# When the attention accumulator takes its PSUM slot, and in which order the second query half visits its key tiles

## The chip, the cores and the metric

The kernel runs on one core of a Trainium2 chip. Five engines work from queues of their own, each in the order in which its instructions were written into the program: TensorE (PE, matrix products and transposes; PEld is its loading of the stationary operand), VectorE (DVE), ScalarE (ACT), GpSimd (POOL) and SyncE (SP, which here only starts DMA transfers). They wait for each other through semaphores. The metric is the time of one execution on the device in microseconds; lower is better.

## The reference

A transformer block in float32 over x of shape (8, 1024, 512): eight batch elements of 1024 tokens. It has two residual branches, each with a layer norm before and after:

```python
x = x + layernorm(attention(layernorm(x)))
x = x + layernorm(feed_forward(layernorm(x)))
```

Attention has 16 heads of 32 columns and a causal mask: q, v, k come from one projection, the weights are softmax((q k^T masked) / sqrt(512)), and the weighted values go through an output projection. The feed-forward part expands 512 to 2048 columns, applies `relu(h + c * w * sin(theta + 0.1 h))` with per-column parameters, and goes back to 512.

## The kernel before

All batch elements are worked one after the other. In each, the 16 heads are taken in four groups of four (`NG`, `HPG`), since four heads of 32 columns fill the 128 rows of TensorE. The tokens are cut into eight tiles of 128 and into two query halves of 512, called `c` in the code.

One head group has two stages. `find_maxima` (line 354) computes scores in nine units, from which DVE takes the row maxima under the causal mask (lines 395 and 400); between its units it lets TensorE advance the projections of the next group (`work`, made by `project_qkv`, tiles `pq` and `pv`). Then `attention` (line 534) walks the ten units of `KEY_UNITS` (line 349): three for the first query half, seven for the second. A unit is one key tile, or two that together fit in 512 columns. For each unit `weigh` (line 430) does this:

- TensorE writes minus the maximum and then the product of keys and queries into two `st` tiles (two heads each).
- ACT takes the exponential into two `w` tiles (line 466) and with that frees the `st` tiles.
- For a key tile on the diagonal, POOL puts zeros where the mask is, one instruction for each `w` tile and each such key tile (line 470). In the first half all units have such tiles: 0, 1 and 3, 2. In the second half these are 4, 5 and 7, 6; key tiles 0 to 3 lie wholly in the past and have none.

The products of a unit with the values (`weighted_values`, line 483) are held back in `late` and issued by `flush`, after the scores of the next unit. They are summed up in a PSUM tile `acc`, plane 0. Plane 1 takes the sums of the weights. In the first half TensorE makes these with a matrix of ones, unit by unit (`weight_sums`, line 496). In the second half DVE adds the weights of all later units onto those of the first one (`add_weights`, line 509; the pair is called `total`), and one sum matmul over this total follows after the scores of the next group's first unit (`sums`). `normalise` (line 516) then divides: DVE transposes the sums, ACT copies the values out and frees `acc`, DVE inverts and multiplies.

PSUM is handled by hand (line 75): four slots of two banks each in a list. A tile takes the slot at the head of the list (`psum`), and puts it at the end when its last reader has been issued (`drained`). So the list fixes, at the time the program is written, which earlier tile's reader a new tile must wait for. Besides `st` and `acc`, the tiles `sc` (scores for the maxima), `pq`, `pv`, `parts_t`, `y`, `xn_t`, `ph` and `ys` all go through this list.

TensorE's queue keeps the order of the source (`keep_in_program_order`), and so do POOL's masks and variance roots (lines 210 and 211). DVE's and ACT's instructions are placed into their queues by the framework's planner when the program is built.

`attention` also runs other work between its units (`more`, from `after` on line 753): in group 0 the rest of the previous element's second residual; in group 2 the first layer norm of the next element (`norm1`: loads into `xin`, statistics, scale, transposes `xn_t`, copies to `xnT`); in group 3, from the second half's second unit on, the first half's `finish_block` (output projection `y`, residual, layer norm, transposes, copies to `x2T`). The feed-forward part follows; its first `ph` matmul reads `x2T`.

The twenty `w` tiles of a group share seven buffers (`pp`), which the feed-forward part uses too.

Of the kernel before, what the change touches and what calls it, by code (L numbers as in the profile page):

```python
# [16 lines left out]
P = 128  # L17
# [14 lines left out]
def kernel(  # L32
# [21 lines left out]
    HALF = 512  # L54
# [23 lines left out]
    def psum(shape, name, dtype=F32):  # L78
        slot = free_slots.pop(0)
        t = ps.tile(shape, dtype, tag=f"s{slot}", name=name)  # L80
        slot_of[id(t)] = slot, t
        return t

    def drained(t):

        free_slots.append(slot_of.pop(id(t))[0])

    def matmul(*args, **kwargs):
        tc.keep_in_program_order(nc.tensor.matmul(*args, **kwargs))  # L89
# [177 lines left out]
    def advance(work, steps=1):  # L267
        for _ in range(steps):
            if next(work, None) is None:
                return  # L270

    def finish(work):
        for _ in work:
            pass
# [26 lines left out]
    def project_qkv(b, g):  # L301


        qk[b, g] = qkp.tile([P, 2, S], F32, tag="qk", name=f"qk_{b}_{g}")
        v[b, g] = vp.tile([P, NT, P], F32, tag="v", name=f"v_{b}_{g}")
        for half in range(2):
            pq = psum([P, 2, HALF], "pq")
            for n, part in enumerate((0, 2)):
                c0 = part * D + g * P
                for kc in range(KC):  # L310
                    matmul(
                        pq[:, n, :],
                        wqvk_sb[:, kc, c0 : c0 + P],
                        xnT[b, half][:, kc, :],
                        start=(kc == 0),
                        stop=(kc == KC - 1),
                    )
                    if kc % 2 and (n, kc) != (1, KC - 1):
                        yield True
            tok = slice(half * HALF, (half + 1) * HALF)  # L320
            nc.scalar.activation(qk[b, g][:, 0, tok], pq[:, 0, :], AF.Copy, scale=QSCALE)
            nc.scalar.copy(qk[b, g][:, 1, tok], pq[:, 1, :])
            drained(pq)
            yield True
        pv = psum([P, NT, P], "pv")
        c0 = D + g * P
        for t in range(NT):
            for kc in range(KC):
                matmul(
                    pv[:, t, :],  # L330
                    xnT[b, t // TPB][:, kc, (t % TPB) * P : (t % TPB + 1) * P],
                    wqvk_sb[:, kc, c0 : c0 + P],
                    start=(kc == 0),
                    stop=(kc == KC - 1),
                )
            if t % 2 and t < NT - 1:
                yield True
        nc.scalar.copy(v[b, g], pv)
        drained(pv)
        yield True  # L340
# [7 lines left out]

    KEY_UNITS = (
        ((0,), (1, 3), (2,)),  # L350
        ((0,), (1,), (2,), (3,), (4,), (5, 7), (6,)),
    )

    def find_maxima(b, g, work, sums):
# [128 lines left out]
    def weighted_values(acc, b, g, first, last, weights, placed):  # L483

        for k, (kb, cols, n) in enumerate(placed):
            for j in range(HPG):
                r = slice(j * HD, (j + 1) * HD)
                matmul(
                    acc[r, 0, HALF - n :],
                    v[b, g][:, kb, r],  # L490
                    weights[j // 2][:, j % 2, cols],
                    start=first and k == 0,
                    stop=last and k == len(placed) - 1,
                )

    def weight_sums(acc, first, last, weights, placed):

        for k, (_, cols, n) in enumerate(placed):
            for j in range(HPG):
                r = slice(j * HD, (j + 1) * HD)  # L500
                matmul(
                    acc[r, 1, HALF - n :],
                    ones,
                    weights[j // 2][:, j % 2, cols],
                    start=first and k == 0,
                    stop=last and k == len(placed) - 1,
                )
# [8 lines left out]
    def normalise(acc, dst):  # L516

        sums = tmp.tile([P, HALF], F32, tag="tmp", name="sums")  # L520
        nc.vector.transpose(sums, acc[:, 1, :])
        nc.scalar.copy(dst, acc[:, 0, :])
        drained(acc)
        yield True
        rinv = small.tile([P, HALF // HD], F32, tag="rinv", name="rinv", bufs=2)
        nc.vector.reciprocal(rinv, sums.rearrange("p (n r) -> p n r", r=HD)[:, :, 0])
        nc.vector.transpose(
            sums.rearrange("p (n r) -> p n r", r=HD),
            rinv.unsqueeze(2).to_broadcast([P, HALF // HD, HD]),
        )  # L530
        nc.vector.tensor_tensor(dst, dst, sums, ALU.mult)
        yield True

    def attention(b, wvT, after):


        late = [None]
        summing = [None]

        def flush():  # L540
            if late[0] is not None:
                late[0]()
                late[0] = None

        def sums():
            if summing[0] is not None:
                summing[0]()
                summing[0] = None

        def projections(g):  # L550
            if g + 1 < NG:
                return project_qkv(b, g + 1)
            if g + 1 == NG and b + 1 < B:
                return project_qkv(b + 1, 0)
            return iter(())

        rests = []

        def settle():
            while rests:  # L560
                finish(rests.pop(0))

        work = projections(0)
        for g in range(NG):
            mTs = [find_maxima(b, g, work, sums)]
            more, first = after(g)
            at = 0
            for c in range(2):
                acc = total = None
                units = KEY_UNITS[c]  # L570
                for u, keys in enumerate(units):
                    weights, placed = weigh(b, g, c, keys, mTs[c])
                    if at == 0:
                        advance(work)
                    if at == 2:
                        mTs.append(transpose_maxima(parts_q[1], nc.vector.tensor_copy))
                    flush()
                    if at:
                        settle()
                    if acc is None:  # L580
                        acc = psum([P, 2, HALF], "acc")

                    if c and u == 0:
                        total = weights, placed
                    elif c:
                        add_weights(total[0], weights, placed)

                    def divide(acc=acc, dst=wvT[c][:, g, :]):  # L590
                        rests.append(normalise(acc, dst))
                        advance(rests[-1])

                    def step(acc=acc, u=u, last=u == len(units) - 1, weights=weights,
                             placed=placed, c=c, g=g, total=total, divide=divide):
                        weighted_values(acc, b, g, u == 0, last, weights, placed)
                        if c == 0:
                            weight_sums(acc, u == 0, last, weights, placed)
                            if last:
                                divide()  # L600
                        elif last:

                            def whole():
                                weight_sums(acc, True, True, *total)
                                divide()

                            summing[0] = whole

                    late[0] = step
                    if at >= first:  # L610
                        advance(more)
                    at += 1
            finish(work)
            work = projections(g + 1)
            advance(work)
            flush()
            if g == NG - 1:
                advance(more)
                sums()
                settle()  # L620
            finish(more)
# [127 lines left out]
    for b in range(B):  # L749
        wvT = [tp.tile([P, KC, HALF], F32, tag="t", name=f"wvT_{b}_{n}") for n in range(2)]  # L750
        x2T = {}

        def after(g, b=b, wvT=wvT, x2T=x2T, rest=rest):

            if g == 0:
                return rest, 1
            if g == NG - 2 and b + 1 < B:
                return norm1(b + 1, True), 0
            if g == NG - 1:
                return finish_block(b, 0, wvT[0], x2T), len(KEY_UNITS[0]) + 1  # L760
            return iter(()), 0
# [47 lines left out]
```

## Time and profile before

| what | value |
|---|---|
| median of three runs | 4212.27 us (4211.95 to 4212.37) |
| the profiled execution's own time | 4213.73 us |
| its span | 4212.0 us |
| busy: PE, DVE, ACT, POOL | 4041.7, 3025.1, 1151.1, 533.1 us |
| mean granted TensorE clock | 0.991 |

The profile is of one execution. A line of its list of groups names the source line and engine, the operation, what it writes and reads, the shapes and the count; then busy time and the mean duration in ns; then the idle time of the engine just before, and what ended it. A line of a timeline gives start and length in us from the span's start, then the engine, line and operation; what stands in brackets at its end is the idle time before it and the instruction that ended it. Matmuls are recorded by one helper (line 89; transposes line 92), so they are told apart by their tiles: `st`, `acc<-w,v`, `acc<-w,ones`, `sc`, `pq`. A table of stretches gives, for each, its length, the busy time of PE, PEld, DVE, ACT and POOL with instruction counts, the granted TensorE clock, the share of DMA and its GB/s.

### The profile page before, as it was taken

How to read it: one execution, taken by the hardware profiler on the slowest of the kernel's cores; microseconds unless marked ns; L12 is line 12 of the kernel's file. 1: busy time of each engine (PE TensorE's matmuls, PEld its weight loads, DVE VectorE, ACT ScalarE, POOL GpSimd, SP SyncE). 2: the span in 40 equal slices, each digit the busy share in tenths (PEclk: the TensorE clock that was granted, in tenths of full speed). 3: DMA queues.
4: the chain of work that ended last, by engine and by line, in shares of the span. 5: the costliest groups of instructions: out<-in, count | busy, mean ns of one | idle time of the engine just before them, and what ended most of it. 6: DMA issues, size and time to landing. Idle time of an engine off the chain costs nothing.

```text
span 4212.0 us, 51995 instructions
## 1 busy us (share of the span) xinstructions
PE 4041.7 (96%) x20481; PEld 1802.6 (43%) x20481; DVE 3025.1 (72%) x6473; ACT 1151.1 (27%) x1564; POOL 533.1 (13%) x1037
## 2 busy tenths in 40 slices
PE   8999999999999999999999999999999999999998
PEld 4434444344443444444444444444444444443343
DVE  5776777766777677776677766777677776777666
ACT  3332123321233212332123321233212432123311
POOL 1121011200112001120011200112001210011100
PEclk9999999999999999999999999999999999999899
DMA  3000000000000000000000000000000000000000
GB/s 138 6 11 10 20 26 7 20 1 20 28 11 13 1 20 28 11 14 1 20 28 14 11 0 20 28 14 11 0 20 28 14 11 0 20 21 11 1 3 18
DMA packets 35430, 71.79 MB, mean 17 GB/s; under 512 B 3248, under 2 KB 3312, under 8 KB 34672
## 3 DMA queue, kind: packets, MB, share of 16 engines
q1 hardware_dynamic: 30992, 56.93, 4.1%
q10 hardware_dynamic: 4192, 11.53, 0.7%
q8 instruction: 160, 2.62, 0.3%
q14 instruction: 86, 0.70, 0.1%
HBM read 51.68 MB, written 16.78 MB: 16 GB/s over the span
## 4 chain that ended last, share of the span: by engine, by line
PE 82%; DVE 9%; POOL 4%; ACT 3%; issue 2%; DMA 0%; ACTq 0%; POOLq 0%; DVEq 0%; SPq 0%
PE ph L89 21%; PE ys L89 21%; PE pq L89 10%; PE sc L89 8%; PE st L89 7%; PE acc L89 6%; PE pv L89 5%; PE y L89 4%; ACT w L466 2%; POOL w L470 2%; DVE w L514 2%; DVE sc L400 1%; DVE st L204 1%; POOL rs L211 1%; PE xn_t L92 1%
## 5 line engine op out<-in xcount | busy, mean ns | idle before, releaser
L89 PE MATMUL ph<-x2T,w_sb 128*128 128x512 f32 x2048 | 921.1, 593 | 12.1 <-ACT hid L682 6.7
L89 PE MATMUL ys<-w_sb,hid 128*128 128x512 f32 x1536 | 691.1, 592 | 0.0
L466 ACT ACTIVATE w<-st 128x1024 f32<-128x1024 f32 (+1 forms) x640 | 565.8, 936 | 313.1 <-PE st L89 299.9
L89 PEld LDWEIGHTS ph<-x2T,w_sb 128*128 128x128 f32 x2048 | 385.3, 190 | 487.5 <-issue 466.8
L470 POOL TENSOR_SCALAR_AFFINE_SELECT w<-w 128x256 f32<-128x256 f32 x512 | 272.4, 553 | 2184.1 <-ACT w L466 2177.9
L400 DVE CUSTOM_DVE_ANT_0 sc<-sc,mask 128x512 f32<-128x512 f32 (+3 forms) x1024 | 487.5, 512 | 53.4 <-PE sc L89 38.9
L89 PE MATMUL pq<-xnT,wqvk_sb 128*128 128x512 f32 x1024 | 497.0, 614 | 1.3
L514 DVE TENSOR_TENSOR w<-w 128x1024 f32<-128x1024 f32 (+3 forms) x448 | 441.4, 1031 | 43.3 <-POOL w L470 29.6
L89 PEld LDWEIGHTS ys<-w_sb,hid 128*128 128x128 f32 x1536 | 291.2, 190 | 368.7 <-issue 341.9
L690 ACT ACTIVATE u<-u 128x512 f32<-128x512 f32 x256 | 161.1, 629 | 883.5 <-DVE u L175 883.4
L89 PE MATMUL sc<-qk 32*128 32x512 f32 (+3 forms) x3072 | 391.2, 529 | 10.3 <-DVE mx L400 6.1
L89 PE MATMUL acc<-w,v 128*32 128x512 f32 (+3 forms) x3072 | 363.8, 503 | 24.6 <-POOL w L470 24.6
L395 DVE TENSOR_REDUCE mx<-sc 128x2 f32<-128x1024 f32 x256 | 301.6, 1217 | 85.0 <-PE sc L89 85.0
L89 PE MATMUL st<-qk 32*128 32x512 f32 (+3 forms) x3072 | 348.8, 507 | 0.0
L685 DVE TENSOR_SCALAR u<-hid,prm 128x512 f32<-128x512 f32 x256 | 123.8, 484 | 292.5 <-ACT hid L682 292.5
L691 DVE SCALAR_TENSOR_TENSOR hid<-u,coef,hid 128x512 f32<-128x512 f32 x256 | 192.0, 750 | 174.0 <-ACT u L690 174.0
L682 ACT ACTIVATE hid<-ph,prm 128x512 f32<-128x512 f32 x256 | 175.4, 685 | 475.7 <-PE ph L89 475.7
L89 PEld LDWEIGHTS pq<-xnT,wqvk_sb 128*128 128x128 f32 x1024 | 176.6, 189 | 275.5 <-issue 247.0
L210 POOL TENSOR_SCALAR rs<-mv 128x1 f32<-128x1 f32 x256 | 78.2, 305 | 1468.3 <-DVE mv L205 1463.3
L89 PEld LDWEIGHTS pv<-wqvk_sb,xnT 128*128 128x128 f32 x2048 | 238.3, 192 | 47.8 <-issue 44.3
L89 PE MATMUL pv<-wqvk_sb,xnT 128*128 128x128 f32 x2048 | 254.4, 279 | 0.0
L89 PE MATMUL st<-mT,minus 32*128 32x512 bf16 (+3 forms) x1536 | 184.8, 333 | 56.4 <-ACT w L466 45.3
(90 smaller groups left out, 3592.9 us busy)
## 6 DMA issues: line engine op xcount, KB each, us to landing
x<-in_L_attn_h_dram SPq DMA_DIRECT2D x64, 256.0 KB, 2.7
out_dram<-x SPq DMA_DIRECT2D x64, 256.0 KB, 2.2
xin<-in_L_attn_h_dram SPq DMA_DIRECT2D x56, 256.0 KB, 2.7
w_tail<-in_L_ffn_W_dram SPq DMA_DIRECT2D x8, 1024.0 KB, 5.0
w_sb<-in_L_ffn_W_dram ACTq DMA_DIRECT2D x1, 4096.0 KB, 14.9
wqvk_sb<-in_L_attn_Wqvk_dram ACTq DMA_DIRECT2D x3, 1024.0 KB, 9.4
w_sb<-in_L_ffn_W_dram ACTq DMA_DIRECT2D x1, 3072.0 KB, 22.1
wo_sb<-in_L_attn_Wo_dram ACTq DMA_DIRECT2D x1, 1024.0 KB, 5.6
```

Source lines behind the costliest of these rows:

```text
L89: tc.keep_in_program_order(nc.tensor.matmul(*args, **kwargs))
L92: tc.keep_in_program_order(nc.tensor.transpose(*args))
L210: tc.keep_in_program_order(nc.gpsimd.tensor_scalar(rs, mv[:, :, 1], EPS, None, ALU.add))
L395: nc.vector.tensor_reduce(out=mx, in_=sc[:, :, cols], op=ALU.max, axis=mybir.AxisListType.X)
L400: nc.vector.tensor_tensor_reduce(out=sc[:, m, cols], in0=sc[:, m, cols], in1=mask[:, HALF - n :], scale=1.0, scalar=-FMAX, op0=ALU.add, op ...
L466: nc.scalar.activation(w[:, :, :width], st[:, :, :width], AF.Exp)
L470: select = nc.gpsimd.affine_select(out=square, in_=square, compare_op=ALU.is_ge, fill=0.0, base=0, pattern=[[0, 2], [1, P]], channel_multi ...
L514: nc.vector.tensor_add(t[:, :, q], t[:, :, q], w[:, :, cols])
L682: nc.scalar.activation(hid, ph, AF.Identity, bias=prm[:, fc : fc + 1])
L685: nc.vector.tensor_scalar(u, hid, 0.1, prm[:, NFC + fc : NFC + fc + 1], ALU.mult, ALU.add)
L690: nc.scalar.activation(u, u, AF.Sin)
L691: nc.vector.scalar_tensor_tensor(hid, u, coef[:, fc : fc + 1], hid, ALU.mult, ALU.add)
```

## The change

Two edits in the attention stage. The tuple of units for the second query half is reordered: the units with diagonal key tiles come first, the four full ones last. And `acc` is no longer taken from the slot list in the loop over units, before its first product is held back, but inside the held-back `step`, when the first unit's products are issued. That is one unit later: the scores of the second unit have taken their slots by then.

```diff
     KEY_UNITS = (
         ((0,), (1, 3), (2,)),
-        ((0,), (1,), (2,), (3,), (4,), (5, 7), (6,)),
+        ((4,), (5, 7), (6,), (0,), (1,), (2,), (3,)),
     )
...
             for c in range(2):
-                acc = total = None
+                accs = []
+                total = None
...
-                    if acc is None:
-                        acc = psum([P, 2, HALF], "acc")
...
-                    def divide(acc=acc, dst=wvT[c][:, g, :]):
-                        rests.append(normalise(acc, dst))
+                    def divide(accs=accs, dst=wvT[c][:, g, :]):
+                        rests.append(normalise(accs[0], dst))
                         advance(rests[-1])
 
-                    def step(acc=acc, u=u, last=u == len(units) - 1, weights=weights,
+                    def step(accs=accs, u=u, last=u == len(units) - 1, weights=weights,
                              placed=placed, c=c, g=g, total=total, divide=divide):
-                        weighted_values(acc, b, g, u == 0, last, weights, placed)
+                        if u == 0:
+                            accs.append(psum([P, 2, HALF], "acc"))
+                        weighted_values(accs[0], b, g, u == 0, last, weights, placed)
                         if c == 0:
-                            weight_sums(acc, u == 0, last, weights, placed)
+                            weight_sums(accs[0], u == 0, last, weights, placed)
                             if last:
                                 divide()
                         elif last:
 
                             def whole():
-                                weight_sums(acc, True, True, *total)
+                                weight_sums(accs[0], True, True, *total)
                                 divide()
 
                             summing[0] = whole
```

The first unit of the second half, whose weights become the total, is now key tile 4 instead of key tile 0. Both span all 512 columns of the half. Sizes and counts of all instructions are the same.

## The prediction

> **What bounds the kernel now.** I read the page first, then TensorE's timeline through one batch element, then the timelines of VectorE (DVE), GpSimd (POOL) and ScalarE (ACT) over the same stretches. TensorE's share on the page is so high that only its own gaps can be won:
>
> ```profile
> PE 4041.7 (96%) x20481; PEld 1802.6 (43%) x20481; DVE 3025.1 (72%) x6473; ACT 1151.1 (27%) x1564; POOL 533.1 (13%) x1037
> L89 PE MATMUL acc<-w,v 128*32 128x512 f32 (+3 forms) x3072 | 363.8, 503 | 24.6 <-POOL w L470 24.6
> L89 PE MATMUL st<-mT,minus 32*128 32x512 bf16 (+3 forms) x1536 | 184.8, 333 | 56.4 <-ACT w L466 45.3
> ```
>
> Batch elements repeat every 521.9 us, so one is enough. TensorE in head group 1 of the second one (weights stage from 660.09, next group's first score at 689.84), start and length in us:
>
> ```profile
> 662.74 0.34 PE L89 MATMUL st<-mT,minus 32*128 32x384 bf16 x2 [1.02 <-ACT w L466]
> ...
> 671.20 0.39 PE L89 MATMUL st<-mT,minus 32*128 32x512 bf16 x2
> 672.12 0.39 PE L89 MATMUL st<-mT,minus 32*128 32x512 bf16 x2 [0.52 <-ACT w L466]
> ...
> 682.59 1.87 PE L89 MATMUL acc<-w,v 128*32 128x512 f32 x8
> ...
> 686.37 1.06 PE L89 MATMUL acc<-w,v 128*32 128x384 f32 x12 [0.48 <-POOL w L470]
> ```
>
> The first two waits are for an exponential to free a score slot: four slots, one held by an accumulator that has no product yet. The 1.87 (undisturbed: 1.07) and the 0.48 are products of units (4) and (5, 7) waiting for POOL's masks. POOL and DVE there:
>
> ```profile
> 665.22 1.68 POOL L470 TENSOR_SCALAR_AFFINE_SELECT w<-w 128x256 f32<-128x256 f32 x4 [1.13 <-ACT w L466]
> ...
> 683.80 4.50 POOL L470 TENSOR_SCALAR_AFFINE_SELECT w<-w 128x256 f32<-128x256 f32 x6 [0.44 <-ACT w L466]
> ```
>
> ```profile
> 674.46 6.97 DVE L514 TENSOR_TENSOR w<-w 128x1024 f32<-128x1024 f32 x6 [0.76 <-PE acc L89]
> ...
> 691.02 2.35 DVE L395 TENSOR_REDUCE mx<-sc 128x2 f32<-128x1024 f32 x2 [1.24 <-PE sc L89]
> ```
>
> A mask costs 0.42 us alone and 0.75 beside DVE's additions. DVE is nearly full: an addition of a full unit is two of 1.16 us against TensorE's 2.33 us per full unit. It waited 1.24 us for the next group's scores, which is its whole slack. In group 2 DVE sets the pace: the transposes wait for its copies; and group 3 ends with a row of short waits:
>
> ```profile
> 1267.52 1.12 PE L92 MATMUL xn_t<-ident,xin 128*128 128x128 f32 x4 [3.79 <-DVE xnT L247]
> ```
>
> ```profile
> 1364.98 1.17 PE L89 MATMUL acc<-w,v 128*32 128x256 f32 x8 [1.01 <-POOL w L470]
> 1366.35 0.63 PE L92 MATMUL xn_t<-ident,xn 128*128 128x128 f32 x4 [0.20 <-DVE xn L215]
> 1366.91 1.60 PE L89 MATMUL acc<-w,ones 128*32 128x512 f32 x8
> ```
>
> **The change, part by part.** No instruction is added or dropped; work is permuted, and the static queues of the built program (which I follow below) move with it. Prices: scores of a full unit 1.32 us, of (5, 7) 1.33, of (6) 0.66; products 1.0, 1.0, 0.5; exponentials 2 x 0.97 (half that for (6)); masks 0.42 each alone; one additions pair 2.3 for a full unit, 3.4 for (5, 7), 1.3 for (6).
>
> *Slot, first half.* In group 1 the second unit's scores no longer stop (1.02 us). But the first unit's products then meet POOL: the second mask ended at 664.08 and the products began at 663.99, so 0.2 us is all that is won. Group 0 wins 0.5 (its stalls of 0.36 and 0.58 go, the mask copy to DVE behind it follows); groups 2 and 3 about 0.
>
> *Slot, second half.* When unit 2 of the second half starts, it finds a slot that nobody holds; the 0.52 and its half-started neighbour go. (5, 7) now sits there: scores 671.1 to 672.5 where they ended at 673.4. From the third unit on three slots rotate as before.
>
> *Masked units first, group 1.* Masks of (4) end at 672.6, its products at 673.5 (before: 674.4). (5, 7): exponentials 672.7 to 674.6 behind ACT's copy of the first half's result, masks to 675.5, products end at 676.2 against 675.1 without any wait. Scores of (0) 676.2 to 677.5, products of (6) 678.0. New wait: the scores of (1) need the slot of (0)'s first exponential, 0.4. Then no masks: (1), (2), (3) follow, projection 1.9, products of (3), and the next score starts at 688.2 instead of 689.84. DVE starts adding at 674.6 (two ops of the divide before), adds 13.8 us without a pause: done 688.4. Sum matmul and maxima need 689.3. So the cover holds by 0.9, and the group wins 1.65 + 0.2, say 1.75.
>
> *Group 0.* The leftover residual work (0.5 scale and 0.65 add per tile) is on DVE too, and POOL's queue now has these tiles' variance roots between the masks: (5, 7) masks end at 611.5, the score of the next group could start at 624.3 (before 627.28), but DVE adds from 612.25 and ends at 627.2. It is late; the sum matmul and the maxima behind it start then, 1.2 before the old 628.45. Win 1.2.
>
> *Group 2.* DVE-bound. Its list from 1262.7: additions 13.9, seven copies 4.3, five scales 2.5, three statistics 2.4, in all 23.1, end 1285.8; the last copy waits for TensorE, 1287.8. The old last one ended at 1288.7. Win 0.9 to 1.0. Loads keep their order and enough lead (4.4 us to landing).
>
> *Group 3.* TensorE is 0.85 ahead at the first output projection and some 1.8 at the fourth. DVE is not: between two projections (5.4 us) it owes 6.3 to 6.7 (statistics, a 0.86 wait for POOL's root, scale, add, 2.3 of additions). At the fourth, (1), (2) and (3) are still owed, 7 us where 4.2 remained before. Additions end at 1367.9, before at 1367.4. TensorE reaches the sum matmul at 1362.5 and waits 5.4; behind it stands the last transpose, and behind that the hidden layer's first matmul: at 1370.2 instead of 1369.78, loss 0.5.
>
> [...] The row first: after the 3.79 us gap of group 2 the granted clock was
>
> ```profile
> core 0: us, PE busy (x) PEld busy (x) DVE busy (x) ACT busy (x) POOL busy (x), PEclk, DMA share, GB/s
> 1264.00:1268.00 4.00, 0.48 (x2) 0.48 (x3) 3.97 (x7) 0.69 (x1) 2.51 (x2) 0.88 0.00 0
> 1268.00:1272.00 4.00, 4.00 (x26) 1.42 (x26) 3.55 (x5) 1.18 (x2) 0.00 (x0) 0.70 0.25 67
> ```
>
> (third number from the end: 0.88, then 0.70), while group 3's end, with gaps of a microsecond, kept 1.00. [...]
>
> [...]
>
> *Sum.* Per element 1.2 + 1.75 + 1.0 - 2.0 = 1.95; eight give 15.6. The first element's group 0 and the last one's group 2 have no neighbour work and behave like group 1: + 0.5 + 0.75. Together 17 us off the profiled execution's 4213.73 (span 4212.0); against the runs' median 4212.27 I say 4195.
>
> **Rivals.**
> (a) *Everything lands.* If DVE keeps up in groups 0 and 3 and the clock stays up: 3.0 (group 0's scores at 624.3) + 1.75 + 2.0 (a third of group 2's 3.79 + 1.86 of waits) + 0 = 6.75 an element, 54 us, 4158. For: TensorE itself would be that early. Against: DVE's list.
> (b) *The wait only changes its name.* If masks at the start of the second half delay products as much as at its end, group wins shrink to 0.5 each, group 3 keeps its loss: 3 x 0.5 - 2.0 = -0.5, 4 us, 4216: no change. For: POOL now has 16 masks in one run. Against: its gaps, and DVE idle beside them.
> (c) *Slower: DVE's full additions come last.* Place: the end of each second half, where sum matmul and maxima queue behind them. Price: in groups 0, 2 and 3 every microsecond that DVE is later than worked out counts whole, in group 1 from 0.9 on. Break-even 0.65 us of extra lateness (3 x 0.65 = 1.95). At 2 us: group 1 +0.6, group 0 -0.8, group 2 -1, group 3 -4, an element -5.2, 41 us, 4253; at 1.3 us 4230. [...] Against: masks beside the divide run at 0.42 to 0.45.
>
> **How the numbers follow.** Forecast 0.42 (4180 to 4206), (a) 0.2, (b) 0.12, (c) 0.26. About 0.2%, 8.4 us, is what a measurement of this kernel can tell. Faster 0.62, same 0.12, slower 0.26. The range, 4160 to 4238, leaves out the outer parts of (a) and (c).
>
> **What would show it.** Right: no ACT wait before the second unit of either half in group 1; DVE's last addition ending about 1 us before the maxima; next score 1.7 us earlier; a gap of about 5 us before group 3's sum matmul, and a granted clock below 1 after it. Wrong: sum matmuls waiting for additions in group 1 too, masks of (5, 7) above 0.7 us each, transposes of group 2 waiting longer in sum than 8 us, or exponentials waiting for weight buffers (seven, two of them held by the total).

## The result, and the profile after

The changed kernel takes 4215.02 us (median of 12 runs, 4213.77 to 4216.68), the kernel before on the same chip 4212.07 us (4209.91 to 4213.42). The ratio is 1.0007, 95% interval 0.9999 to 1.0016: no change. 4195 was forecast, with 0.62 on faster. The case that came true in its time, "same", had 0.12, though not for its reason.

The page of the profiled execution (span 4215.0 us): the engines, the masks, the products that wait for them and the hidden layer's first matmuls. Below it, two of these groups in the kernel before:

```profile
PE 4046.5 (96%) x20481; PEld 1808.3 (43%) x20481; DVE 3011.4 (71%) x6473; ACT 1147.4 (27%) x1564; POOL 473.4 (11%) x1037
L470 POOL TENSOR_SCALAR_AFFINE_SELECT w<-w 128x256 f32<-128x256 f32 x512 | 233.9, 474 | 2245.6 <-ACT w L466 2228.1
L89 PE MATMUL acc<-w,v 128*32 128x512 f32 (+3 forms) x3072 | 360.3, 502 | 18.4 <-POOL w L470 18.3
L89 PE MATMUL ph<-x2T,w_sb 128*128 128x512 f32 x2048 | 932.5, 599 | 12.1 <-ACT hid L683 6.7
```

```profile
L470 POOL TENSOR_SCALAR_AFFINE_SELECT w<-w 128x256 f32<-128x256 f32 x512 | 272.4, 553 | 2184.1 <-ACT w L466 2177.9
L89 PE MATMUL ph<-x2T,w_sb 128*128 128x512 f32 x2048 | 921.1, 593 | 12.1 <-ACT hid L682 6.7
```

Two things matter here. Masks became cheaper (474 ns each, before 553), and TensorE's waits for them shrank from 24.6 to 18.4 us. But the hidden layer's matmuls, which the change never touches, take 932.5 us where they took 921.1: the same 2048 instructions run longer.

TensorE in group 1 of the second element, the stretch shown in the prediction (this stage starts at 661.29, before 660.09):

```profile
664.48 1.54 PE L89 MATMUL acc<-w,v 128*32 128x512 f32 x6 [0.46 <-POOL w L470]
...
672.27 0.52 PE L89 MATMUL st<-mT,minus 32*128 32x384 bf16 x4
...
676.81 1.06 PE L89 MATMUL acc<-w,v 128*32 128x384 f32 x12 [0.42 <-POOL w L470]
...
680.23 0.39 PE L89 MATMUL st<-mT,minus 32*128 32x512 bf16 x2 [0.29 <-ACT w L466]
...
689.87 1.14 PE L89 MATMUL sc<-qk 32*128 32x512 f32 x8
```

Both waits for a slot are gone. In the first half a wait for POOL stands in the place of the old one; in the second half the masked unit still waits 0.42, and the foreseen wait of the unit after the short one is there (0.29). VectorE beside it, the additions in one piece and then the maxima, which waited for the scores and not the scores for them:

```profile
676.79 12.64 DVE L514 TENSOR_TENSOR w<-w 128x768 f32<-128x768 f32 x13 [0.30 <-POOL w L470]
691.05 2.36 DVE L395 TENSOR_REDUCE mx<-sc 128x2 f32<-128x1024 f32 x2 [1.62 <-PE sc L89]
```

The end of group 3 in the third element on TensorE, and the granted clock (third number from the end) over the same time, in stretches cut where the clock changes:

```profile
1361.64 0.66 PE L92 MATMUL xn_t<-ident,xn 128*128 128x128 f32 x4
1366.48 3.06 PE L89 MATMUL acc<-w,ones 128*32 128x512 f32 x8 [4.18 <-DVE w L514]
1369.47 1.12 PE L92 MATMUL xn_t<-ident,xn 128*128 128x128 f32 x4
1371.26 5.37 PE L89 MATMUL ph<-x2T,w_sb 128*128 128x512 f32 x8 [0.68 <-ACT x2T L247]
```

```profile
1361.01:1364.42 3.41, 1.29 (x10) 0.42 (x4) 2.74 (x4) 0.66 (x2) 0.49 (x2) 1.00 0.65 237
1364.42:1367.83 3.41, 1.34 (x6) 0.38 (x8) 2.81 (x3) 0.00 (x0) 0.30 (x1) 0.50 0.00 0
1367.83:1371.24 3.41, 2.76 (x10) 0.71 (x4) 1.58 (x3) 0.61 (x2) 0.00 (x0) 0.50 0.00 0
1371.24:1374.66 3.42, 3.40 (x4) 1.50 (x5) 0.79 (x2) 0.46 (x1) 0.00 (x0) 0.50 0.01 2
1374.66:1378.07 3.41, 2.57 (x7) 0.93 (x6) 0.58 (x2) 0.69 (x1) 0.00 (x0) 1.00 0.00 0
```

TensorE waits 4.18 us for the additions. The clock falls to 0.50 in that wait, at 1364.42, and is back at 1.00 at 1374.66, after 10.24 us. These cover the end of the wait, the sum, the transpose, one more wait of 0.68 and most of the eight hidden matmuls, which take 5.37 us. At 1.00 they take 3.70 (kernel with the transpose before the sum, below).

From such timelines I cut every element in pieces: for each group from the first score of the weights stage to the next score (group 3: to the first hidden matmul), and the rest of the element, which is the feed-forward part and the first maxima stage. Means over elements 2 to 7, in us (the maxima stages of groups 1 to 3 are the same in all these kernels, within 0.06, except where said):

| kernel | group 0 | group 1 | group 2 | group 3 | rest |
|---|---|---|---|---|---|
| before | 33.57 | 29.75 | 40.73 | 49.40 | 269.18 |
| changed | 31.46 | 28.58 | 41.13 | 51.32 | 270.69 |
| slot only | 33.50 | 28.85 | 40.33 | 48.43 | 269.18 |
| order only | 32.98 | 29.50 | 42.26 | 52.19 | 269.72 |
| group 3 in the old order | 31.46 | 28.58 | 40.50 | 48.43 | 269.18 |
| nine unread matmuls | 31.46 | 28.58 | 40.75 | 52.41 | 269.16 |
| six unread matmuls | 31.44 | 28.58 | 41.15 | 50.05 | 269.16 |
| transpose before the sum | 31.46 | 28.58 | 41.27 | 49.30 | 269.15 |
| last sums on TensorE, group 3 | 31.46 | 28.58 | 40.64 | 46.40 | 269.15 |
| groups 2 and 3 in the old order | 31.46 | 28.58 | 40.02 | 48.42 | 269.17 |
| last sums on TensorE, groups 2 and 3 | 31.45 | 28.58 | 40.17 | 46.40 | 269.16 |
| as this, one unit of group 2 | 31.45 | 28.58 | 40.44 | 46.40 | 269.16 |

Groups 0 and 1 win 3.3 us an element; group 3 and the rest lose 3.4; group 2 loses 0.4. That is the whole result.

### The profile page after: what moved, and what is told of

Its sections match the earlier page's. It is cut to its first block, busy times and chain, and to the rows that moved or that the text cites. A ratio compares the mean times of both kernels' runs of the same rounds, so it can differ in the third digit from the quotient of the medians.

```text
span 4215.0 us, 52012 instructions
## 1 busy us (share of the span) xinstructions
PE 4046.5 (96%) x20481; PEld 1808.3 (43%) x20481; DVE 3011.4 (71%) x6473; ACT 1147.4 (27%) x1564; POOL 473.4 (11%) x1037
## 4 chain that ended last, share of the span: by engine, by line
PE 83%; DVE 9%; POOL 3%; ACT 3%; issue 2%; DMA 0%; POOLq 0%; ACTq 0%; SPq 0%; DVEq 0%
PE ph L89 21%; PE ys L89 21%; PE pq L89 10%; PE sc L89 8%; PE acc L89 7%; PE pv L89 5%; PE st L89 5%; PE y L89 4%; DVE w L514 3%; ACT w L466 2%; DVE sc L400 1%; DVE st L204 1%; POOL rs L211 1%; POOL w L470 1%; PE xn_t L92 1%
## 5 line engine op out<-in xcount | busy, mean ns | idle before, releaser
L89 PE MATMUL ph<-x2T,w_sb 128*128 128x512 f32 x2048 | 932.5, 599 | 12.1 <-ACT hid L683 6.7
L470 POOL TENSOR_SCALAR_AFFINE_SELECT w<-w 128x256 f32<-128x256 f32 x512 | 233.9, 474 | 2245.6 <-ACT w L466 2228.1
L89 PE MATMUL acc<-w,v 128*32 128x512 f32 (+3 forms) x3072 | 360.3, 502 | 18.4 <-POOL w L470 18.3
L89 PE MATMUL st<-qk 32*128 32x512 f32 (+3 forms) x3072 | 339.3, 504 | 0.0
L89 PEld LDWEIGHTS sc<-qk 32*128 32x128 f32 x3072 | 145.8, 186 | 214.9 <-DVE mx L400 79.5
```

What stands on the lines that cost most here:

```text
L470: select = nc.gpsimd.affine_select(out=square, in_=square, compare_op=ALU.is_ge, fill=0.0, base=0, pattern=[[0, 2], [1, P]], channel_multi ...
```

## The experiments

My theory (theory 1 in the expectations) was that group 3 gives back what groups 0 and 1 win: VectorE's full additions come last there, TensorE waits long for them, and the clock falls in that wait. The main rival was that the loss comes from the late slot, or that the clock is only a by-product.

**Slot only.** The changed kernel with the old tuple of units.

```diff
-        ((4,), (5, 7), (6,), (0,), (1,), (2,), (3,)),
+        ((0,), (1,), (2,), (3,), (4,), (5, 7), (6,)),
```

> Only the late slot, the old order of units. Theory 1 (group 3's loss comes from the full additions at the end, not from the slot): no long wait before group 3's sum matmul, clock there 1.00, feed-forward as before (269.2 us); groups 0 and 1 win what the stalls of 0.5 to 1 us in the second half were worth, 0.7 to 1.0 each; about 4197 us (4190 to 4205). Rival (every slot win is paid back to the masks of the same stretch): no change, 4212 within 4.

Measured 4189.54 us (before 4213.1), ratio 0.9945, interval 0.9931 to 0.9960. Faster, and more than expected. The place differs: on the mean group 0 wins nothing by the slot alone (33.50), group 1 wins 0.9, and group 3, where I had put about nothing, wins 1.0. The rest is unchanged. The slot is not what costs. Group 0's mean hides two values: 32.97 in four of the six elements, a gain of 0.6, and 34.55 in two, where the granted clock was 0.50 for 3.41 us in the middle of the stage.

**Order only.** The kernel before with the new tuple of units.

> Only the new order, the slot as before. Theory 1: group 3 loses 3 to 4 us an element exactly as with both parts (stage 51.3, feed-forward 270.7), groups 0 and 1 win 0.5 to 1.5 each, less than with both; about 4222 us (4214 to 4230). Rival (the two parts only lose together, because the late slot brings TensorE too early to the masks): no loss in group 3, 4200 or below.

Measured 4245.66 us, ratio 1.0077 (1.0062 to 1.0092): slower, and by more than expected. Group 3 loses 2.8 and the rest 0.5, as theory 1 says of it in the main; group 2 loses 1.5, which it did not say. Group 0 wins only 0.6 and group 1 0.25. The rival falls: group 3 loses without the late slot too. The two parts do not add: -23.6 and +32.6 would make +9 us, where both together make +3 in one comparison. The table shows where they help each other: group 0, -0.1 and -0.6 alone, -2.1 together, and group 2, -0.4 and +1.5 alone, +0.4 together. The rest goes the other way (0 and 0.5 alone, 1.5 together). Why the order alone costs group 2 that much I did not follow further.

**Group 3 in the old order.** Both parts, with the old tuple for group 3.

```diff
         ((4,), (5, 7), (6,), (0,), (1,), (2,), (3,)),
+        ((0,), (1,), (2,), (3,), (4,), (5, 7), (6,)),
...
-                units = KEY_UNITS[c]
+                units = KEY_UNITS[2 if c and g in (3,) else c]
```

> Both parts, but group 3 keeps the old order of units. Theory 1: group 3 goes back to 49.4 us or less and the feed-forward part to 269.2, so 8 x 3.4 to 3.7 less: about 4186 us (4180 to 4192), faster than both kernels. Rival (the feed-forward part's 1.5 us come from slot numbers or a queue's order, not from group 3's end): feed-forward stays at 270.7, 4199.

Measured 4178.1 us, ratio 0.9917 (0.9902 to 0.9932): faster than both kernels, and by 8 us more than expected, because group 3 does not go back to 49.4 but to 48.43, its value with the slot alone. The rest returns to 269.18, so its loss was group 3's end and not slot numbers.

**Nine unread matmuls.** To take the clock apart from the lateness, TensorE gets work in its wait; its result goes to a PSUM slot that is not read.

```diff
                 advance(more)
+                warm = psum([P, 2, HALF], "warm")
+                for i in range(9):
+                    matmul(warm[:, i % 2, :], wo_sb[:, 0, :P], wo_sb[:, 0, :], start=True, stop=True)
+                drained(warm)
                 sums()
```

> Both parts, and nine matmuls (128x512) into a PSUM slot that nobody reads, in front of group 3's last sum matmul, where TensorE waits 4.2 us. Theory 1 (the granted clock falls in that wait and stays down for some 9 us): clock 1.00, feed-forward back to 269.2, sum matmul and last transpose at 1.0 and 0.66 us; some 2.5 an element less than both parts alone: 4195 us (4190 to 4200). Rival (only VectorE's lateness counts, the clock is a by-product): 4215 within 4.

Measured 4212.14 us, ratio 0.9996 (0.9987 to 1.0005): not the 4195 of theory 1 but within the rival's range. As a time it decides nothing, since the filler was sized wrongly. TensorE at that place in the third element:

```profile
1359.58 7.89 PE L89 MATMUL warm<-wo_sb 128*128 128x512 f32 x18
1367.40 1.06 PE L89 MATMUL acc<-w,ones 128*32 128x512 f32 x8
1368.39 0.66 PE L92 MATMUL xn_t<-ident,xn 128*128 128x128 f32 x4
```

Each of the nine is two instructions of 0.44 us, 7.89 us in all, while the last addition ended at 1365.0. The sum matmul comes 2.4 us late by the filler alone. Yet the rest is back at 269.16, and sum and transpose are at 1.06 and 0.66.

**Six unread matmuls.** As above with `range(6)`.

> Both parts with six unread matmuls instead of nine in front of group 3's last sum matmul. Nine took 7.89 us (two passes of 0.44 each) and ran 2.5 us past the last addition; six take 5.3 and end with it. Theory 1 (clock): clock 1.00, stage of group 3 49.8 to 50.0 instead of 51.3, feed-forward 269.2 instead of 270.7, 3 us an element less than both parts alone: 4191 us (4187 to 4196). Rival (the feed-forward part gains only because the stage before it ends later): stage stays above 51, 4205 or more.

Measured 4189.67 us (before 4211.68), ratio 0.9946 (0.9930 to 0.9963), as theory 1 had it. The stage is 50.05, the rest 269.16: 1.27 + 1.53 = 2.8 us an element against the changed kernel, for work that does nothing. Granted clock over the 12 us around the first hidden matmul of the third element, in the kernel before, the changed one and this one (the second line of the changed kernel is its fourth element):

```profile
1363.78:1375.78 12.00, 9.28 (x38) 3.60 (x37) 7.84 (x16) 2.93 (x5) 2.77 (x5) 1.00 0.11 39
```

```profile
1365.26:1377.26 12.00, 9.47 (x20) 3.16 (x20) 4.68 (x7) 1.60 (x3) 0.00 (x0) 0.61 0.00 1
1888.73:1900.73 12.00, 8.85 (x24) 3.02 (x25) 6.47 (x11) 1.76 (x3) 0.00 (x0) 0.86 0.00 0
```

```profile
1355.52:1367.52 12.00, 10.49 (x33) 4.16 (x32) 6.56 (x11) 1.76 (x3) 0.70 (x2) 1.00 0.00 1
```

The changed kernel's own elements agree. At group 3's end the clock is at 0.50 for 10.24 us in six of the eight, and there the rest of the element takes 1.65 to 2.23 us more than in the kernel before. In the fourth it is low for 3.41 us, in the eighth for 6.83, and there the rest is undisturbed (269.16; the eighth's 249.42, against 249.44 with group 3 in the old order). In the fourth the low stretch begins 0.3 us before the wait ends:

```profile
1886.67:1890.08 3.41, 0.00 (x0) 0.00 (x0) 2.41 (x4) 0.14 (x1) 0.79 (x2) 1.00 0.11 41
1890.08:1893.49 3.41, 3.12 (x9) 0.52 (x10) 1.39 (x3) 0.00 (x0) 0.00 (x0) 0.50 0.00 0
```

**Transpose before the sum.** In group 3 the last transpose no longer stands behind the sum matmul.

```diff
             if g == NG - 1:
-                advance(more)
+                finish(more)
                 sums()
```

> Both parts, but in group 3 the last transposes are issued before the last sum matmul, so that the hidden layer's first matmul no longer stands behind all additions. Theory 1: TensorE waits for the last tile's scale instead (some 3 us instead of 4.2), the clock falls less often, and the first hidden matmul comes 1 to 3 us earlier; 4195 us (4188 to 4208). Rival (the sum matmul then stalls the hidden layer in the same way, behind it in the queue): 4215 within 5.

Measured 4186.95 us, ratio 0.9942 (0.9927 to 0.9956), a little better than the range of theory 1. The stage is 49.30 and the rest 269.15. The rival falls, since the copy of the transpose now runs beside the sum matmul. The wait is not gone:

```profile
1357.42 1.09 PE L92 MATMUL xn_t<-ident,xn 128*128 128x128 f32 x4 [3.13 <-DVE xn L215]
1358.46 2.78 PE L89 MATMUL acc<-w,ones 128*32 128x512 f32 x8
1361.17 3.70 PE L89 MATMUL ph<-x2T,w_sb 128*128 128x512 f32 x8
```

Here the wait is 3.13 us, the transpose and the sum still run slow (1.09, 2.78), but the clock is low for 3.41 us only (1357.43 to 1360.84) and up again before the hidden matmuls (3.70).

**Last sums on TensorE.** In group 3 TensorE sums the weights of the last two full units itself, 16 matmuls more, and VectorE adds only the others.

```diff
-                    elif c:
+                    elif c and not (g == NG - 1 and u >= 5):
                         add_weights(total[0], weights, placed)
...
+                            mine = list(ones_of)
+                            ones_of.clear()
                             def whole():
-                                weight_sums(accs[0], True, True, *total)
+                                for n, (w, at_) in enumerate(mine):
+                                    weight_sums(accs[0], n == 0, False, w, at_)
+                                weight_sums(accs[0], not mine, True, *total)
...
+                    if c and g == NG - 1 and u >= 5:
+                        ones_of.append((weights, placed))
                     late[0] = step
```

> Both parts, but in group 3 the sums of the last two full units are made by TensorE (16 matmuls of 128x512 more an element, 2 us) and VectorE is spared their additions (4.7 us). Theory 1 (VectorE's list sets group 3's end): the 4.2 us wait shrinks to about nothing, clock 1.00, the stage about 50, feed-forward 269.2: 4190 us (4184 to 4197). Rival (TensorE's own work sets it): 2 us an element more, 4231.

Measured 4161.76 us, ratio 0.9883 (0.9868 to 0.9898): the fastest of all, 50 us under the kernel before. The stage is 46.40, 3.6 less than expected.

```profile
1344.62 0.66 PE L92 MATMUL xn_t<-ident,xn 128*128 128x128 f32 x4
1345.21 2.78 PE L89 MATMUL acc<-w,ones 128*32 128x512 f32 x24
1347.92 0.66 PE L92 MATMUL xn_t<-ident,xn 128*128 128x128 f32 x4
1349.25 3.70 PE L89 MATMUL ph<-x2T,w_sb 128*128 128x512 f32 x8 [0.68 <-ACT x2T L247]
```

No wait is left between the transposes. 1.7 us more of TensorE buys the 4.2 us wait and the clock's price. Why the stage fell so far below the expected 50 was not followed further.

**Groups 2 and 3 in the old order.** As group 3 in the old order, with `g in (2, 3)`.

> Both parts, groups 2 and 3 with the old order. Theory (group 2's order is worth about 1 us when the clock holds and nothing on the mean, since stretches at low clock eat it): within 3 us of the kernel with the old order in group 3 alone, 4178 (4174 to 4183). Rival (the new order costs group 2 as the mean of the changed kernel suggested, 0.4): 4175 or less.

Measured 4173.39 us, ratio 0.9908 (0.9894 to 0.9923), below the theory's range and in the rival's. Against the kernel with group 3 alone in the old order (0.9917) the difference is not clear of the intervals. In the profiles group 2 takes 40.02 on the mean against 40.50, but the shortest elements of both take 39.75: the order itself costs nothing there, and what differs is how often the longer values come (see group 2 below).

**Sums on TensorE in groups 2 and 3**, and **one unit of group 2**: as "last sums on TensorE", with `g >= NG - 2 and u >= 5`, and with `u >= 8 - g`.

> As the kernel with the last two units' sums on TensorE, now in groups 2 and 3. Theory 1 (VectorE's list sets the pace of group 2 as well): group 2's stage falls from 40.6 on the mean to about 38 (4.7 us less on VectorE, 2 more on TensorE), no element above 40, 7 x 2.5 less: 4144 us (4136 to 4154). Rival (the transposes' chain through copies and variance roots sets it, not VectorE's load): 40.6 plus the 2 us of TensorE, 4176.

> As before it, but in group 2 only the last unit's sums on TensorE (1 us, VectorE spared 2.35). Theory 1: group 2 about 39.3 on the mean, 4152 us (4145 to 4160). Rival as above: 4168.

Measured 4171.38 us (before 4211.34; ratio 0.9905, 0.9890 to 0.9920) and 4165.48 us (0.9889, 0.9873 to 0.9906). Both are near the rival. The first is slower than with group 3 alone (4161.76); the second's 4165.48 is not clear of it, since their runs overlap. Group 2's stage hardly moves (40.17 and 40.44 against 40.64), and the maxima stage behind it grows by TensorE's 1.7 and 0.9. VectorE at the end of group 2 in the first of them:

```profile
1266.11 0.68 DVE L247 COPY xnT<-xn_t 128x512 f32<-128x512 f32 x1
1267.54 0.69 DVE L247 COPY xnT<-xn_t 128x512 f32<-128x512 f32 x1 [0.75 <-PE xn_t L92]
1271.95 0.69 DVE L247 COPY xnT<-xn_t 128x512 f32<-128x512 f32 x1 [3.72 <-PE xn_t L92]
```

VectorE now stands idle for 3.72 us there and TensorE is what it waits for. So my reading that VectorE's whole list sets group 2's end is wrong. TensorE loses its time earlier: in the third element it waits four times for copies that queue behind additions, 1.02, 1.73, 2.30 and 2.63 us in this kernel and the same within 0.01 in the one with group 3 alone. The last two units' additions come after the last copy that it waits for.

## Why the prediction was wrong, step by step

- *Slot, first half.* The mechanism is right (a wait for POOL takes the place of the wait for the slot), the size a little off: nothing won in group 1 instead of 0.2. Up to the third unit's scores that stage takes 5.95 us, before 5.89.
- *Masked units first, group 1.* Right in kind: no slot wait, masks at 0.41 beside the divide, a new wait after the short unit, additions ahead of the sum matmul. 1.75 was forecast, 1.17 measured. The 0.75 us that the prediction reads for a mask beside additions is a mean of two kinds. A mask that starts outside an addition mostly takes 0.41 (0.40 to 0.43 in 409 of 452 in the changed kernel, in 329 of 380 before). One that starts inside an addition ends about 0.27 after the addition's end (all 60 such masks of the changed kernel, 122 of the 132 before), like this one of the kernel before:

```profile
681.86 1.22 DVE L514 TENSOR_TENSOR w<-w 128x1024 f32<-128x1024 f32 x1 [0.43 <-POOL w L470]
682.34 1.02 POOL L470 TENSOR_SCALAR_AFFINE_SELECT w<-w 128x256 f32<-128x256 f32 x1 [0.51 <-ACT w L466]
```

  In the stretch shown, only one of the four masks of (5, 7) started inside an addition (0.93 us, the others 0.41), so little of this delay came.
- *Group 0.* 1.2 was forecast, 2.1 measured. I had VectorE's additions late for the sum matmul by nearly two microseconds. They end with the scores: counted from the stage's start, 0.8 us earlier than I had them, and TensorE comes 0.9 later (masks of the short unit hold it 0.67 us). The larger gain was luck, and it hid part of what the next points lost.
- *Group 2, -1.0.* This step failed: +0.4. The forecast was worked from the third element, whose stage of 42.38 us was the longest of that execution (mean 40.73). Two low stretches of the clock lie in it, of which the prediction's rows caught the first:

```profile
1267.01:1270.42 3.41, 2.90 (x16) 1.38 (x16) 3.38 (x6) 0.00 (x0) 0.28 (x1) 0.50 0.20 47
1277.24:1280.66 3.42, 3.42 (x32) 1.68 (x33) 2.95 (x4) 0.48 (x1) 2.24 (x2) 0.50 0.00 0
```

  The shortest element of before takes 39.78, that of the changed kernel 39.76 (mean granted clock 0.96 in both): there the new order wins nothing. The changed kernel's other elements take 41.0 to 41.3, one 42.5, with the same instructions. What differs is where the low stretch falls. In the kernel with group 3 in the old order (group 2 as in the changed kernel), element 2 (39.76) and element 3 (41.19), the low stretch and TensorE's last wait for a copy in each:

```profile
743.62:747.03 3.41, 3.13 (x16) 1.38 (x16) 2.95 (x5) 0.00 (x0) 2.15 (x3) 0.50 0.00 0
1265.86:1269.27 3.41, 3.37 (x20) 1.45 (x24) 2.86 (x3) 0.00 (x0) 0.00 (x0) 0.50 0.00 0
```

```profile
749.37 0.66 PE L92 MATMUL xn_t<-ident,xin 128*128 128x128 f32 x4 [1.16 <-DVE xnT L247]
1265.90 1.12 PE L92 MATMUL xn_t<-ident,xin 128*128 128x128 f32 x4 [2.63 <-DVE xnT L247]
```

  Both waits end 33.0 us into the stage. In the first element the low stretch lies before the wait, which is shorter for it (1.16 instead of 2.63), so the lost time is taken up. In the other it lies behind the wait and costs 1.4 us. The stages start at 716.36 and 1232.90, so the stretches begin 27.3 and 33.0 us into them. This is a reading of the traces; no run held the clock up in group 2.
- *Group 3, loss 0.5 by VectorE's lateness.* Right: with the clock held up the stage is 50.05, before 49.40, a loss of 0.65. Against the same kernel with the old order in group 3 (48.43) the order costs 1.6; the late slot, for which I had put nothing in this group, wins 1.0.
- *Group 3, 1.5 for the clock.* No run shows this term of the 2.0 for group 3; it was my estimate, and in its place the runs show 2.8 (1.27 in the stage, 1.53 in the rest). This is the step that failed, together with group 2. The direction was right: in TensorE's wait, 4.2 us where I had 5.4, the granted clock falls to 0.50, where the trace of before has 1.00 at this place. But the size was not: the second row of group 2 in the prediction, 4 us at 0.70, is worth 1.2 us at full clock, while here the clock stayed at 0.50 for 10.24 us in six of eight elements. In the third element TensorE was busy for 1.34, 2.76 and 3.40 us of the three stretches of 3.41 at 0.50, and the clock was at 1.00 after the third; in the fourth element it was busy for 3.12 us of the first, and the clock was at 1.00 after that one. In the last element TensorE was busy through a whole stretch at 0.50 (3903.94 to 3907.35), and the next was at 0.50 too, so these rows make no rule. Nor did it take a wait as long as 4.18 us: in the transpose-before-sum kernel the clock was at 0.50 from the end of a wait of 3.13.
- *The sum.* -1.2 - 1.75 - 1.0 + 2.0 = -1.95 was forecast; -2.1 - 1.2 + 0.4 + 1.9 + 1.5 = +0.5 is measured. The gains of groups 0 and 1 came together near the forecast (2.95 and 3.3). Groups 2 and 3 were each 1.4 us an element worse than forecast, and that is the miss. Rival (b) had the time, by another way; rival (c), the additions, named the place. Against the old order in group 3 they cost 1.6 us an element and the clock 2.8.

## What to carry to other kernels

When work is moved towards the end of a stage, look for the longest single wait that this leaves on TensorE: here a wait of 4.18 us cost 2.8 us more than itself (against the kernel with six unread matmuls), 1.5 of them in the feed-forward part, which had not been touched. Before working from one repetition of a loop, see how long the others take: group 2 was worked from the slowest one, and a part of its time was the clock's. A change that helps some repetitions of a loop and hurts one can be applied by repetition: the same two edits without the new order in one group of four gave 0.8%, and moving two sums to the engine that waits gave 1.2%. Relieving an engine that looks full paid here only in front of the instruction that somebody waited for: in group 3 it did (stage 51.32 to 46.40), in group 2 the same edit won nothing (40.64 to 40.17, and the maxima stage behind it 1.7 longer).

## What was not expected of the hardware

In the changed kernel, with waits of 4.18 to 4.19 us at the end of group 3, the granted clock was at 0.50 for 10.24 us in six of eight elements, though TensorE was working for 7.5 of them (third element); with a wait of 3.13 us, in the transpose-before-sum kernel, it was at 0.50 for 3.41 us (third element). The changed kernel's trace has 17 stretches at 0.50: six of 3.41 us, two of 6.83, seven of 10.24, and one each of 23.89 and 12.67 in the last element. Their starts lie whole multiples of one step apart, all 17 within 0.01 us, such as 842.18 and 1364.42 (522.24 us) or 1364.42 and 1890.08 (525.66). Worked out from these two distances as 153 and 154 steps, the step is 3.413 us. From one group 2 stage to the next there are 521.6 to 522.8 us, 152.8 to 153.2 steps, so the same wait falls at another place between these starts each time, and group 2 took 39.8, about 41.2 or 42.5 us in elements of one execution, with nothing between. That this place is the cause is a reading of the traces. In the transpose-before-sum kernel the second to the seventh element take 518.78 to 518.88 us, about 152 steps (518.8), and there group 2 takes 41.2 to 41.3 us in every element but the last. A mask that started beside one of VectorE's additions ended 0.27 us after it (all 60 of the changed kernel); elsewhere it mostly took 0.41 (409 of 452).
